# A graph layer on one core: its instruction queues planned with transfers that land later

## The chip, the cores and the metric

The kernel runs on one core of a Trainium2 chip. The core has five instruction queues that matter here: TensorE (PE, with its weight loads, PEld), VectorE (DVE), ScalarE (ACT), GpSimd (POOL) and SyncE (SP, which issues most transfers). The metric is the device time in microseconds (us). Each time given for a kernel is the median of several executions; one more execution, profiled, gives the page and the trace.

## The reference

The reference is one layer of a graph network on 64 graphs of 256 nodes with 256 channels, added to its input:

```
h     = relu(layernorm(x))
x_conv = relu(conv2(relu(conv1(h))) + h)       # over the nodes; conv1 has 1 tap, conv2 17
s     = h @ w_se.T + b_se                      # 3 columns
A     = exp(-|s_n - s_m|^2) * adj
x_nmp = A @ relu(h @ w_msg.T + b_msg)
gi    = [x_conv, x_nmp] @ w_ih.T + b_ih;  gh = h @ w_hh.T + b_hh
r, z  = sigmoid(gi_r + gh_r), sigmoid(gi_z + gh_z)
n     = tanh(gi_n + r * gh_n)
out   = x + (1 - z) * n + z * h
```

The adjacency is 64 x 256 x 256. Everything is float32.

## The kernel before

**Tiling.** The graphs are taken in 32 pairs; four pairs make a block, and there are eight blocks. For a block, the 17-tap convolution is done in a transformed domain: vector instructions (`Fft`, lines 48 to 228) transform the blocks U and V, TensorE multiplies each frequency with a filter matrix (`product`, 935), which a 256 KB transfer from the DRAM tile `filt` brings to one of nine slots `wb0` to `wb8` (`load_kinds`, 910), and vector instructions transform back (`branch_back`, `odd_back`, `q_back`, `p_back`, `join`). The gates of a pair are computed with seven products of quarter matrices instead of eight (`seven`, 1162), whose sums are partly built on TensorE's accumulators by ScalarE and VectorE: `acc<-acc` is line 1167, `acc<-acc,wb` is line 1176, and `wb<-Yv`, `wb<-hT`, `wb<-xnm` are the operand sums of `sums` (1104). Between the two halves of a pair's gates, and around them, stand the steps of other pairs (1426 to 1513).

**Data that arrives by transfer.** Layernorm's statistics of a later pair are taken on VectorE from rows in `x` (`stats`, 745, instruction `st<-x`). Its normalized rows go to `hh` by ScalarE (`turn_h`, 810), are transposed by a transfer into `halves`, sorted back to `hh` by four more (`sort_h`, 821) and copied by ScalarE to a tile of the ring `hT` (`join_h`, 828). The adjacency goes a similar way: `turn_adj` (631), `load_adj` (638) and, on ScalarE, `join_adj` (648) with the copies `adj<-adjh`. A finished pair is transposed by a transfer from `back` to `gn` (`finish`, 1266), copied by ScalarE (`deliver`, 1287, `back<-gn`), and then GpSimd's queue adds the input rows and writes out. So ScalarE's `hT<-hh`, `adj<-adjh` and `back<-gn` and VectorE's `st<-x` each read what a transfer has brought; the other instructions of these two engines mostly feed TensorE.

**What sets the order.** No instruction goes to the chip when its line is run. `Recorder.record` (334) stores it as a task with a planned cost, a transfer's planned share of the DMA engines (`size`), and its predecessors, found from overlapping memory. `plan` (395) then puts the tasks in order, and `emit` (470) issues them in that order, each engine's queue in the order of its own tasks. The program calls `emit` twice: at line 1376 (851 tasks, the first 150 us or so) and at line 1514 (10245 tasks: 4181 tensor, 3106 vector, 2039 scalar, 735 sync, 184 gpsimd).

`plan` gives each task a due time, `late`. TensorE's tasks have theirs from their order in the program, by adding up planned costs; the others' follow backwards from the tasks that need them. Then it plays the engines forward: an engine takes what can start first, and among what can start at that time, the task that is due first. A task can start when its predecessors are done and the lag between the engines has passed. A transfer is taken to move at 1.6 us after its issue or when the DMA engines are through with what was planned before, for `size`, and to be seen 1.1 us after that. At most eight transfers per issuing queue are under way at once in the plan. One rule treats tasks that are not urgent in another way: a transfer of SP whose due time is more than `CALM` = 20 us ahead of TensorE's place in the plan (`pace`) waits until the DMA engines are nearly free.

All instructions pass through `record`, so the profile gives them its line 378 (374 for some joined matmuls), and they are told apart by their tiles.

Of the kernel before, what the change touches and what calls it, by code (L numbers as in the profile page):

```python
# [249 lines left out]
class Recorder:  # L250
# [144 lines left out]
    def plan(self, fixed=False):  # L395

        T, new = self.tasks, range(self.planned, len(self.tasks))
        self.planned = len(T)
        total = 0.0
        for k in new:  # L400
            t = T[k]
            for p in t.preds:
                T[p].succs.append(k)
            if t.engine == "tensor":
                t.late = total
                total += t.cost
        for k in reversed(new):
            t = T[k]
            for s in t.succs:
                t.late = min(t.late, T[s].late - self.lag(t, T[s]) - self.cost(t))  # L410
            if t.first is not None:
                t.late = t.first - 1e6
        ready, free = {e: [] for e in self.LAG}, self.free
        left = {}

        def enable(k):
            at = max((T[p].done + self.lag(T[p], T[k]) for p in T[k].preds), default=0.0)
            ready[T[k].engine].append((at, k))
        for k in new:
            left[k] = sum(p in left for p in T[k].preds)  # L420
            if not left[k]:
                enable(k)
        order = []
        self.pace = 0.0

        def when(e, at, t):
            now = max(free[e], at)
            if t.size:
                now = max(now, self.lanes[e == "gpsimd"][0])
                if e != "gpsimd" and self.pace + self.CALM < t.late < math.inf:  # L430
                    now = max(now, self.dma - 1.0)
            return now

        def commit(k, e, at, now):
            t = T[k]
            ready[e].remove((at, k))
            t.begin = now
            free[e] = t.done = now + t.cost
            if e == "tensor":
                self.pace = max(self.pace, t.late)  # L440
            if t.size:
                if t.cost == self.TURN:
                    free[e] = max(free[e], self.dma + 1.1)
                self.dma = max(self.dma, now + 1.6) + t.size
                t.done = self.dma + 1.1
                lanes = self.lanes[e == "gpsimd"]
                lanes.popleft()
                lanes.append(t.done)
            order.append(k)
            for s in t.succs:  # L450
                left[s] -= 1
                if not left[s]:
                    enable(s)
        while fixed and len(order) < len(new):
            k = new[len(order)]
            e = T[k].engine
            at = next(at for at, j in ready[e] if j == k)
            commit(k, e, at, max(free[e], at, self.lanes[e == "gpsimd"][0] if T[k].size else 0.0))
        while len(order) < len(new):
            best = []  # L460
            for e in ready:
                cand = [(when(e, at, T[k]), T[k].late, k, at) for at, k in ready[e]]
                if cand:
                    now = min(cand)[0]
                    best.append((now, min(c[1:] for c in cand if c[0] <= now + 1e-9), e))
            now, (_, k, at), e = min(best)
            commit(k, e, at, now)
        return order
# [1091 lines left out]
```

## Time and profile before

| | us |
|---|---|
| time, median of 3 executions | 1669.88 (1669.51 to 1676.13) |
| the profiled execution | 1671.57 |
| its span | 1669.8 |
| TensorE busy | 1652.6 (99%) |
| VectorE busy | 1459.3 (87%) |
| ScalarE busy | 1148.6 (69%) |
| GpSimd busy | 242.5 (15%) |

The profiled execution is the slowest core's, and there is only one core. Busy time counts the time in which an engine executes; the ends of matmuls are modelled, so a busy TensorE may still run below its best. In a row of the timeline, the first number is the start, the second the time until the last of the grouped instructions ended, then engine, operation, `out<-in` by tile names and shapes, how many were grouped (`x`), and, in brackets, how long the engine was idle before it and what ended that. 261.39 MB are moved in the span, 157 GB/s on the mean.

### The profile page before, as it was taken

The page shows a single profiled execution, that of the slowest core. Times are in us where ns is not written, and L with a number is a line of the kernel's source. Part 1 is how long each engine was busy: PE and PEld are TensorE (multiplying, and loading weights), DVE is VectorE, ACT ScalarE, POOL GpSimd, SP SyncE. Part 2 cuts the span into 40 slices and gives each one's busy share as a digit, 9 for nine tenths or more (in the row PEclk, how much of TensorE's full clock was granted, in tenths as well). Part 3 has the DMA queues.
Part 4 walks back from the last instruction along what each step waited for, and adds up shares of the span by engine and source line. Part 5 has one row for each costly group of instructions (what it writes and reads, how often), then busy time and mean ns, then how long its engine had stood idle before and what let it go on. Part 6 is the DMA issues. An engine that isn't in the chain of part 4 may idle for free.

```text
span 1669.8 us, 26552 instructions
## 1 busy us (share of the span) xinstructions
PE 1652.6 (99%) x9008; PEld 1417.0 (85%) x9008; DVE 1459.3 (87%) x3391; ACT 1148.6 (69%) x2157; POOL 242.5 (15%) x245
## 2 busy tenths in 40 slices
PE   9999999999999999999999999999999999999999
PEld 6898778988899788988789887898889978898887
DVE  7979979899799997899888997989979899789645
ACT  5556676776767767686676777677676776667655
POOL 4211410013110131102110031001311013000010
PEclk9999999999999999999999999999999999999999
DMA  9982557846578455873568645784647835465022
GB/s 253 312 293 69 105 128 204 262 103 146 118 204 225 101 127 126 240 203 94 101 145 259 158 95 120 177 259 102 148 111 201 240 94 127 110 218 149 19 57 57
DMA packets 314938, 261.39 MB, mean 157 GB/s; under 512 B 192875, under 2 KB 240263, under 8 KB 314802
## 3 DMA queue, kind: packets, MB, share of 16 engines
q1 hardware_dynamic: 297010, 216.71, 49.1%
q0 software_dynamic: 17376, 42.66, 11.1%
q8 instruction: 71, 1.16, 0.3%
q14 instruction: 65, 0.53, 0.1%
q10 hardware_dynamic: 416, 0.32, 0.1%
HBM read 156.60 MB, written 43.78 MB: 120 GB/s over the span
## 4 chain that ended last, share of the span: by engine, by line
PE 79%; DVE 12%; DMA 4%; issue 2%; ACT 1%; SPq 1%; POOL 1%; ACTq 0%; DVEq 0%
PE acc L378 50%; PE aux L378 28%; DVE V L378 3%; DVE T L378 2%; DMA hh<-halves 2%; DVE Yv L378 2%; DVE wb L378 1%; DMA x<-in_x_dram 1%; PE aux L374 1%; DVE e L378 1%; SPq L378 1%; DMA wb<-filt 1%; POOL shift L378 1%; DVE msg L378 1%; DVE st L378 0%
## 5 line engine op out<-in xcount | busy, mean ns | idle before, releaser
L378 PE MATMUL acc<-wb,w_ih 128*128 128x256 f32 x768 | 189.9, 382 | 0.0
L378 PEld LDWEIGHTS acc<-wb,w_ih 128*128 128x128 f32 x768 | 146.0, 191 | 22.1 <-issue 2.3
L378 POOL DMA_DIRECT2D back<-in_x_dram x62 | 56.7, 1059 | 735.1 <-ACT back L378 594.1
L378 POOL TENSOR_TENSOR rstd<-rstd,neg_half 128x4 f32<-128x4 f32 x32 | 79.3, 2478 | 432.4 <-DVE shift L378 275.5
L378 DVE SCALAR_TENSOR_TENSOR V<-T,V 128x128 f32<-128x128 f32 (+2 forms) x448 | 141.5, 384 | 0.0
L378 ACT COPY back<-tr 128x512 uint16<-128x512 uint16 x124 | 130.4, 1078 | 15.7 <-DVE tr L378 15.3
L378 PE MATMUL aux<-wb,w_x 128*128 128x256 f32 x576 | 137.5, 381 | 2.6 <-DVE wb L378 2.6
L378 PE MATMUL acc<-wb,w_x 128*128 128x256 f32 x576 | 135.1, 380 | 0.0
L378 PEld LDWEIGHTS aux<-wb,w_x 128*128 128x128 f32 x576 | 108.7, 190 | 22.6 <-DVE wb L378 5.4
L378 PEld LDWEIGHTS acc<-wb,w_x 128*128 128x128 f32 x576 | 109.0, 190 | 18.6 <-issue 1.9
L378 PEld LDWEIGHTS acc<-U,wb 128*128 128x128 f32 x1024 | 118.3, 192 | 1.8 <-DMA wb<-filt 0.4
L378 PE MATMUL acc<-U,wb 128*128 128x128 f32 x1024 | 119.2, 275 | 0.3 <-DMA wb<-filt 0.3
L378 PE MATMUL aux<-w_msg,hT 128*128 128x259 f32 x512 | 118.6, 381 | 0.0
L378 PE MATMUL acc<-V,wb 128*128 128x128 f32 x1024 | 118.5, 275 | 0.0
L378 PEld LDWEIGHTS acc<-V,wb 128*128 128x128 f32 x1024 | 116.4, 192 | 0.5 <-DMA wb<-filt 0.5
L378 PE MATMUL acc<-wb,w_hh 128*128 128x256 f32 x384 | 105.7, 384 | 5.1 <-DVE acc L378 2.8
L378 DVE TENSOR_TENSOR e<-e,adj 128x256 f32<-128x256 f32 x128 | 68.7, 596 | 46.7 <-ACT e L378 46.7
L378 PEld LDWEIGHTS aux<-w_msg,hT 128*128 128x128 f32 x512 | 95.9, 190 | 14.1
L378 PE MATMUL aux<-hT,w_c 128*128 128x512 f32 x224 | 106.7, 600 | 0.3
L378 PE MATMUL acc<-Yv,w_ih 128*128 128x256 f32 x380 | 103.2, 381 | 2.1 <-ACT Yv L378 2.1
L378 PE MATMUL acc<-hT,w_hh 128*128 128x256 f32 x380 | 105.1, 383 | 0.0
L378 PE MATMUL acc<-xnm,w_ih 128*128 128x256 f32 x380 | 104.0, 380 | 0.0
(218 smaller groups left out, 3909.2 us busy)
## 6 DMA issues: line engine op xcount, KB each, us to landing
wb<-filt SPq DMA_DIRECT2D x348, 256.0 KB
back<-in_x_dram POOLq DMA_DIRECT2D x62, 256.0 KB, 5.3
out_dram<-back POOLq DMA_DIRECT2D x62, 256.0 KB, 3.1
x<-in_x_dram SPq DMA_DIRECT2D x58, 256.0 KB
halves_d<-halves SPq DMA_DIRECT2D x28, 512.0 KB
adjh<-halves_d SPq DMA_DIRECT2D x112, 128.0 KB
hh<-halves SPq DMA_DIRECT2D x108, 128.0 KB
filt<-Yv POOLq DMA_DIRECT2D x18, 224.0 KB, 4.3
```

The lines of the kernel that those rows point to most:

```text
L374: self.tasks[k].call.append(lambda: method(*args, **kw))
L378: self.tasks.append(Task(engine, [lambda: method(*args, **kw)], cost, size, self.first))
```

## The change

The planner's picture of transfers is altered in the second emission only (`new[0]` is the number of the first task of an emission; it is 0 in the first). A transfer is planned as done 2.1 us after its share of the DMA engines, instead of 1.1. And where a task that is no transfer itself has a due time more than 20 us ahead of TensorE's place, at the moment at which its last predecessor is planned, the transfers among its predecessors count as done another 3.0 us later. Nothing else is touched: the same instructions with the same operands are issued, in an order that comes out of the altered plan. Since a planned transfer keeps its place among the eight until it is done, these places are held 1.0 us longer too.

```diff
@@ -414,7 +414,8 @@
         left = {}
 
         def enable(k):
-            at = max((T[p].done + self.lag(T[p], T[k]) for p in T[k].preds), default=0.0)
+            calm = 3.0 if new[0] and not T[k].size and self.pace + self.CALM < T[k].late < math.inf else 0.0
+            at = max((T[p].done + (calm if T[p].size else self.lag(T[p], T[k])) for p in T[k].preds), default=0.0)
             ready[T[k].engine].append((at, k))
         for k in new:
             left[k] = sum(p in left for p in T[k].preds)
@@ -442,7 +443,7 @@
                 if t.cost == self.TURN:
                     free[e] = max(free[e], self.dma + 1.1)
                 self.dma = max(self.dma, now + 1.6) + t.size
-                t.done = self.dma + 1.1
+                t.done = self.dma + (2.1 if new[0] else 1.1)
                 lanes = self.lanes[e == "gpsimd"]
                 lanes.popleft()
                 lanes.append(t.done)
```

## The prediction

> **What bounds the kernel now.** Read first: the busy row of the page and the shares of the chain that ended last.
>
> ```profile
> PE   1652.6 (99%) x9008; PEld 1417.0 (85%) x9008; DVE 1459.3 (87%) x3391; ACT 1148.6 (69%) x2157; POOL 242.5 (15%) x245
> PE 79%; DVE 12%; DMA 4%; issue 2%; ACT 1%; SPq 1%; POOL 1%; ACTq 0%; DVEq 0%
> ```
>
> TensorE is busy for 1652.6 of 1669.8 us, and the change adds and removes no instruction. So it can only win or lose the time in which TensorE stands still or runs slowly. DVE at 87% and ACT at 69% matter only where TensorE waits for them. Which waits involve data that lands late? The list of waits:
>
> ```profile
> ACT back L378 <- DMA gn<-back: 16.3, 10, 3.1
> DVE st L378 <- DMA x<-in_x_dram: 12.3, 9, 3.9
> ACT hT L378 <- DMA hh<-halves: 4.8, 6, 1.7
> PE acc L378 <- DVE acc L378: 2.8, 3, 1.9
> PE aux L378 <- DVE wb L378: 2.6, 6, 0.5
> PE acc L378 <- ACT acc L378: 2.4, 1, 2.4
> ```
>
> The columns are total us, times, longest. DVE and ACT wait for transfers; TensorE hardly waits for transfers, but waits for DVE and ACT. The timeline joins the two. Near 812 us, DVE and then PE:
>
> ```profile
> 809.83 0.43 DVE L378 BATCH_NORM_STATS2 st<-x 128x6 f32<-128x256 f32 x1 [2.68 <-DMA x<-in_x_dram]
> 811.57 0.69 DVE L378 SCALAR_TENSOR_TENSOR acc<-acc,wb 128x512 f32<-128x512 f32 x1
> ```
>
> ```profile
> 809.40 1.02 PE L378 MATMUL aux<-hT,w_c 128*128 128x512 f32 x2
> 812.32 0.70 PE L378 MATMUL acc<-wb,w_hh 128*128 128x256 f32 x2 [1.90 <-DVE acc L378]
> 814.18 1.06 PE L378 MATMUL aux<-hT,w_c 128*128 128x512 f32 x1
> ```
>
> A statistics instruction whose result is wanted in a much later pair heads DVE's queue, waits 2.68 us for its rows, and `acc<-acc,wb`, which TensorE wants at once, stands behind it. Then a second price: at 809.40 two 512-wide matmuls take 1.02 us, at 814.18 one takes 1.06. The windows (us, busy time of PE, PEld, DVE, ACT, POOL, then granted clock, DMA share, GB/s) show why:
>
> ```profile
> 200.00:212.00 12.00, 9.61 (x38) 7.80 (x38) 11.68 (x38) 9.55 (x17) 5.73 (x4) 0.88 0.65 121
> 812.00:820.00 8.00, 7.68 (x25) 5.23 (x26) 7.70 (x17) 4.37 (x11) 0.00 (x0) 0.79 0.64 123
> ```
>
> The granted clock is 0.79 over 8 us after that stall, so (1 - 0.79) x 8 = 1.7 us of clock at most. The same on ACT near 208 us:
>
> ```profile
> 199.44 1.35 ACT L378 COPY back<-gn 128x1024 uint16<-128x1024 uint16 x1 [1.60 <-DMA gn<-back]
> 202.54 1.36 ACT L378 COPY hT<-hh 128x1024 uint16<-128x1024 uint16 x1 [1.74 <-DMA hh<-halves]
> 203.75 0.68 ACT L378 ACTIVATE tr<-acc,b_rz 128x512 f32<-128x512 f32 x1
> 207.38 0.60 ACT L378 ACTIVATE acc<-acc 128x512 f32<-128x512 f32 x1
> ```
>
> Two copies of landed data wait 1.60 and 1.74 us; `acc<-acc`, for which TensorE stands from 205.4 to 208.0, comes after them. A small form recurs in every block of four pairs, some 199 us apart (ACT, DVE and PE near 551 us):
>
> ```profile
> 532.00 1.36 ACT L378 COPY hT<-hh 128x1024 uint16<-128x1024 uint16 x1 [0.69 <-DMA hh<-halves]
> ```
>
> ```profile
> 550.32 0.69 DVE L378 TENSOR_TENSOR wb<-Yv 128x512 f32<-128x512 f32 x1
> ```
>
> ```profile
> 551.07 1.13 PE L378 MATMUL aux<-wb,w_x 128*128 128x256 f32 x4 [0.52 <-DVE wb L378]
> ```
>
> **The size of what can be had.** I took each matmul's distance from the end of the one before and subtracted the median distance of its shape. What is left above that, at places over 0.3 us after the first emission: 2.66 at 208.0; 0.47 at 415.0; 2.17 at 812.3, then 0.42, 0.43 and 0.35 in the slow clock; 0.91 at 1012.9; 2.36 and 0.57 at 1541.7; and eight small ones at 544.5, 551.1, 748.4, 943.7, 950.3, 1148.8, 1340.5, 1347.1 (0.36 + 0.78 + 0.55 + 0.37 + 0.78 + 0.78 + 0.37 + 0.78 = 4.77). All together 15.1 us, 0.9% of the kernel.
>
> **What the Trainium skill says.** "TensorE: Matmul & The Clock Gate", section "Architectural detail", has ScalarE and VectorE take their queues strictly in order: the trace agrees, 2.68 us of waiting passed on to the instruction behind. Its section "What's actually happening" has the clock fall to half for a window of 3413 ns after too little activity: three spells of half clock, 3.413 us each, start at 209.1, 813.2 and 1543.7, each just behind a stall of over 2 us; stalls under 1 us have none. "DMA: Bandwidth & Descriptors", section "Latency and other measured facts", puts the access time of HBM at 0.2 us on average and 2 us under high load, so that a fixed landing time in a plan must be wrong at times: the rows for 809.83 were issued at 802.5, 7.3 us before, with the DMA engines 91% busy.
>
> **The change, part by part.** In the second emission (after about 150 us) the plan lets every transfer land 1.0 us later, and lets an instruction whose due time is more than 20 us away count the transfer 3.0 us later still. Only orders change; no wait is added but what the new orders bring. Laid side by side, the lists of the two kernels differ in place for 1298 of 3106 vector, 1074 of 2039 scalar, 440 of 735 sync, 536 of 4181 tensor and 26 of 184 gpsimd tasks. The 4.0 us of both together exceed every wait in the three DMA rows above (3.9, 3.1, 1.7).
>
> *812 and 1013 us.* The statistics and two transform steps move 24 DVE places back, behind the n gate's chain; `acc<-acc,wb` now follows one sum. It could start by about 809.8, when PE has just issued its last ready matmul: stall gone (2.17), and the slow clock with it (0.42 + 0.43 + 0.35 = 1.20). At 1012.9 the 1.42 us wait of the same statistics is replaced likewise: 0.91. Sum -4.3. The statistics run later, but their result feeds a pair that is tens of us away. At 415 the order is as before: 0.
>
> *208 us.* `tr<-acc,b_rz` (its operand is ready at 199.35) moves ahead of the copies: 199.4 to 200.6. The hT copy still waits to 202.54, then 1.36 + 0.64 (message relu, moved forward) + 1.34 + 1.35 less overlaps of 0.1 each: `acc<-acc` starts near 207.1 and ends 207.7, only 0.3 earlier; PE has one more conv1 matmul pair (0.86 us) to fill with. Between 1.1 (stall shortened) and 2.66 + 1.5 of clock (gone): I take 1.3, since the wait for hh stays.
>
> *Every block.* The hT copies move 28 and 15 ACT places back, one adj copy and one back copy 20; the copies V<-acc and the exponentials come first. Taking out the 0.69 wait and the 1.36 copy ahead of V<-acc, DVE's back transform starts near 536.4 instead of 537.7 and `wb<-Yv` ends near 549.5 instead of 551.0, while PE wants it at 550.3. I take 4.0 of the 4.77, as 1 in 6 may stay. hT is first wanted by matmuls tens of us after (its copy would end by about 543), which hides the move; without that cover each late copy costs up to 1.36.
>
> *SP.* Four hh loads (0.6 us of issue each) move 6 places back behind filter loads, and transpositions (3.75 us of issue) 8; the filter loads move 1 to 3 places forward and none gets a new long wait in front. adjh loads move 10 to 20 back. POOL: two places at most. I price this at 0; if a filter load were delayed, its cover is 7.2 us (issued 521.67, used 528.84).
>
> *1541 us.* Orders nearly equal from 1510 on: 0.
>
> *New stalls.* 1298 moved DVE tasks at 87% load will not all be free. Bounds: 0, and 1.2 us in each of seven blocks (the slower rival). I take +1.5.
>
> Sum: -4.3 - 1.3 - 4.0 + 1.5 = -8.1. The profiled execution took 1671.57 us (span 1669.8 and 1.8 around it) and would take 1663.5; the median of the three runs is 1669.88, 1.7 less, so **1661.8**.
>
> **Rivals.** (a) *Most of the moves reorder hidden work.* Only the two statistics stalls go (-4.3) and new small ones give 1 to 3 back: 1666 to 1669. For it: DVE's 87% leave it little room to catch up within a block. (b) *No effect*: the real landings, not the planned order, set the waits, and the instructions merely wait in other places: 1669.9. Against: the waiting instruction does stand 24 places later. (c) *Slower: SP's queue.* The hT copies leave hh about 12 us later, so the next fill of hh and its transposition wait on SP (the profile has SP waiting 111.4 us for ACT's hh in 15 places, up to 15.5), with filter loads behind them. The cover of a filter load is 7.2 us, of which its own landing takes about 3 (an estimate from the page's 3.1 us median for the equally large out_dram writes); a transposition of 3.75 us in front uses up the rest. Beyond that each us of delay is a us of TensorE, once in each of seven blocks. From 8.1 / 7 = 1.2 us per block it eats the gain; at 2.4 it gives 1669.9 - 8.1 + 16.8 = 1678.6. Against: filter loads stand earlier in SP's list, not later. (d) *All goes*, clock spells at 208 and 812 included: -4.3 - 4.2 - 4.8 = 1656.6.
>
> **From cases to numbers.** A difference of 0.5% (8.3 us, so 1661.5 and 1678.2) is about what a measurement of this kernel tells from none: the three runs lie within 0.4%. Chances: my forecast (most stalls go, own range 1657 to 1666) 0.56, (d) 0.09, (a) 0.15, (b) 0.07, (c) or a like new stall 0.13. The forecast's centre lies just on the faster bound, so somewhat under six tenths of it count as faster: 0.56 x 0.58 + 0.09 = 0.42; slower takes most of (c), 0.10, and same the rest, 0.48. The range 1656 to 1674 leaves out the low end of (d) and the strong half of (c).
>
> **What would show it.** Right: the wait of st for x and of ACT's copies shrink to a few us; PE shows no wait at 812, 1013, 551, 748, 950, 1148, 1347; no clock under 0.9 around 812; 208 shorter; 1541 unchanged. Wrong: a new PE wait in every block (for DVE wb, ACT h or DMA wb), more SP wait for ACT hh, or the same statistics wait with TensorE behind it at another time.

## The result, and the profile after

The changed kernel takes 1657.57 us (median of four executions, 1654.78 to 1658.67), the kernel before, with the runs of that session, 1672.91 us (1669.51 to 1676.13). The ratio is 0.9906, 95% interval 0.9877 to 0.9935: faster by 0.9%. The profiled execution took 1657.88 us with a span of 1656.1, 13.7 us less than before.

The page of the changed kernel, busy row and shares of the chain that ended last:

```profile
PE 1645.5 (99%) x9008; PEld 1416.7 (86%) x9008; DVE 1458.7 (88%) x3391; ACT 1150.6 (69%) x2157; POOL 242.6 (15%) x245
PE 96%; DVE 2%; DMA 2%; ACT 0%; issue 0%; SPq 0%; DVEq 0%; ACTq 0%
```

The work is the same (9008 matmul records, 3391 on DVE, 2157 on ACT). The chain went from PE 79% and DVE 12% to PE 96% and DVE 2%: it now hardly ever leaves TensorE. From the list of waits of the changed kernel (total us, times, longest), the rows on late data and TensorE's own:

```profile
ACT back L378 <- DMA gn<-back: 17.0, 8, 2.5
DVE st L378 <- DMA x<-in_x_dram: 4.0, 2, 3.6
PE acc L378 <- ACT Yv L378: 2.1, 1, 2.1
PE acc L378 <- DMA wb<-filt: 1.2, 2, 1.0
ACT hT L378 <- DMA hh<-halves: 0.7, 1, 0.7
PE aux L378 <- DVE wb L378: 0.3, 1, 0.3
```

Two of the three DMA rows shrank (st from 12.3 to 4.0, both of these waits before 350 us; hT from 4.8 to 0.7). The third did not: ACT still waits 17.0 us for `gn<-back`, before 16.3. But TensorE's rows for DVE acc and ACT acc are gone, and its row for DVE wb fell from 2.6 to 0.3. ScalarE's waits for `gn` no longer have anything urgent behind them, and cost TensorE nothing here. The place that was at 812 us, now at 802, DVE and then PE:

```profile
801.65 0.68 DVE L378 TENSOR_TENSOR wb<-hT 128x512 f32<-128x512 f32 x1
802.25 0.69 DVE L378 SCALAR_TENSOR_TENSOR acc<-acc,wb 128x512 f32<-128x512 f32 x1
```

```profile
802.85 0.59 PE L378 MATMUL aux<-Yv,w_x 128*128 128x256 f32 x2
803.28 0.59 PE L378 MATMUL acc<-wb,w_hh 128*128 128x256 f32 x2
```

No statistics stand ahead of `acc<-acc,wb`; the matmul that needs it starts 0.43 us after the one before, its usual spacing. Near 208 us, ScalarE:

```profile
200.91 0.69 ACT L378 ACTIVATE tr<-acc,b_rz 128x512 f32<-128x512 f32 x1 [1.80 <-issue]
202.84 1.35 ACT L378 COPY hT<-hh 128x1024 uint16<-128x1024 uint16 x1 [0.66 <-DMA hh<-halves]
206.99 0.63 ACT L378 ACTIVATE acc<-acc 128x512 f32<-128x512 f32 x1
```

The gate activation goes ahead of the hT copy, as forecast, and `acc<-acc` still ends only at 207.6. The windows of these two places:

```profile
200.00:212.00 12.00, 12.00 (x54) 9.91 (x53) 12.00 (x41) 9.45 (x16) 3.09 (x4) 1.00 0.50 113
798.00:806.00 8.00, 8.00 (x35) 6.32 (x34) 8.00 (x19) 3.40 (x8) 0.56 (x1) 1.00 0.86 223
```

PE is busy throughout and the granted clock is 1.00 (0.88 and 0.79 before).

**Where the 13.7 us are.** The measure of the prediction (each matmul's distance from the end of the one before, less the median of its shape, summed over distances more than 20 ns above it) gives, by stretch of the span:

| excess, us | to 150 | 150 to 1500 | from 1500 | sum |
|---|---|---|---|---|
| before | 6.9 | 32.7 | 6.7 | 46.2 |
| changed | 8.0 | 17.9 | 6.7 | 32.5 |

All the gain, 14.8 us, lies between 150 and 1500 us, and there not one place of the changed kernel is over 0.3 us above its own matmuls' spacing, small joined ones apart; what is left, about 0.6 us per 50, is mainly these (`aux<-zT`, the same in both kernels). By place: 812 with its clock 3.4, 1013 0.9, 415 0.5, the eight small ones of the blocks 4.8, the 50 us from 200 on 4.2: 13.8, and 1 us of smaller ones. The stretch to 150 us is the first emission, whose plan the change doesn't touch; its 1.1 us more are late filter loads, which differ from run to run (6.5 to 9.5 us in eleven of thirteen profiles).

### The profile page after: what moved, and what is told of

The parts are those of the page before. It is cut to its first block, busy times and chain, and to the rows that moved or that the text cites. A ratio compares the mean times of both kernels' runs of the same rounds, so it can differ in the third digit from the quotient of the medians.

```text
span 1656.1 us, 26512 instructions
## 1 busy us (share of the span) xinstructions
PE 1645.5 (99%) x9008; PEld 1416.7 (86%) x9008; DVE 1458.7 (88%) x3391; ACT 1150.6 (69%) x2157; POOL 242.6 (15%) x245
## 4 chain that ended last, share of the span: by engine, by line
PE 96%; DVE 2%; DMA 2%; ACT 0%; issue 0%; SPq 0%; DVEq 0%; ACTq 0%
PE acc L378 58%; PE aux L378 37%; DMA wb<-filt 1%; PE aux L374 1%; DVE V L378 0%; DVE T L378 0%; DMA T<-in_x_dram 0%; DVE st L378 0%; DVE Yv L378 0%; DVE wb L378 0%; ACT h L378 0%; DVE e L378 0%; ACT Sv L378 0%; ACT T L378 0%; DVE hh L378 0%
## 5 line engine op out<-in xcount | busy, mean ns | idle before, releaser
L378 POOL TENSOR_TENSOR rstd<-rstd,neg_half 128x4 f32<-128x4 f32 x32 | 75.7, 2366 | 399.3 <-DVE shift L378 261.2
L378 PEld LDWEIGHTS aux<-wb,w_x 128*128 128x128 f32 x576 | 108.9, 191 | 15.7 <-DVE wb L378 1.0
L378 PE MATMUL aux<-e,msg 128*128 128x256 f32 x448 | 104.7, 379 | 0.0
```

The source lines that it names most:

```text
L378: self.tasks.append(Task(engine, [lambda: method(*args, **kw)], cost, size, self.first))
```

## The experiments

The table gives the time, the ratio to the kernel before, run beside it on the same chip, and the excess of TensorE between 150 and 1500 us. The kernel before has 32.7 there and the changed one 17.9.

| kernel | median us | ratio, 95% interval | excess 150 to 1500 |
|---|---|---|---|
| only statistics put back | 1665.82 | 0.9958 (0.9940 to 0.9977) | 25.1 |
| only row loads put forward | 1668.20 | 0.9965 (0.9948 to 0.9982) | 24.4 |
| landing alone | 1658.82 | 0.9905 (0.9874 to 0.9937) | 20.2 |
| 3.0 us for what is not urgent, alone | 1664.94 | 0.9954 (0.9934 to 0.9974) | 24.6 |
| ACT's order alone | 1727.52 | 1.0316 (1.0277 to 1.0355) | 81.6 |
| ACT's and DVE's order | 1685.99 | 1.0072 (1.0049 to 1.0095) | 47.1 |
| ACT's, DVE's and PE's order | 1658.46 | 0.9907 (0.9884 to 0.9931) | 18.5 |
| changed, landing 3.1 | 1661.10 | 0.9926 (0.9898 to 0.9953) | 23.6 |
| changed, last block edited, first try | 1657.82 | 0.9908 (0.9888 to 0.9927) | 17.9 |
| changed, last block edited, mended | 1656.79 | 0.9902 (0.9887 to 0.9916) | 17.7 |

One more kernel, with extra instructions that make stalls of known length, was executed once, with the profiler (1683.48 us). It is read by its trace alone and has no row in the table.

In several of these kernels, the second emission makes both plans and takes each engine's queue from one of them; the queues are then issued in any order that keeps the predecessors:

```diff
+        for self.soft in (False, True):
...
+            order = self.plan()
+            for e in self.LAG:
+                if self.soft == (e in self.TAKE):
+                    queues[e] = [k for k in order if self.tasks[k].engine == e]
...
+        self.edit(queues)
```

`soft` switches the two edits of the change; `TAKE` names the engines that get the changed kernel's order.

**Theory A**: a transfer that lands later than planned stops the instruction that reads it; this one stands at the head of an in-order queue, and what TensorE needs stands behind. **Rival B**: the new orders of TensorE and of the transfers carry the gain.

### Moving one kind of reader, or one kind of transfer

The queues of the kernel before, first with five statistics instructions moved, then with six pairs of transfers swapped:

```diff
+        q = queues["vector"]
...
+            if self.op[q[n]][0] == "bn_stats" and op == "scalar_tensor_tensor" and out.tensor.space == bass.MemoryType.PSUM:
+                q.insert(n + 24, q.pop(n))
```

```diff
+        q = queues["sync"]
...
+            if name[n:n + 7] == ["turn halves", "x"] + 4 * ["hh"] + ["x"]:
+                q[n], q[n + 1] = q[n + 1], q[n]
```

> All five queues in the order of the kernel before; only in VectorE's, the first statistics of a pair moves 24 places back wherever the sum acc<-acc,wb stands four places behind it (five places in the kernel: near 412, 610, 810, 1010 and 1208 us). Theory A (a late landing is passed on to TensorE through the head of an in-order queue): the stalls at 415 (0.47), 812 (2.17, and 1.20 of slow clock) and 1013 (0.91) go, 4.8 us, ratio 0.9971; the stalls at 208 and in every block (551 and its like) stay. Rival B (the gain comes from the new orders of TensorE and SP, and the waits of VectorE are only a symptom): no change, ratio 1.000, or the statistics wait turns up elsewhere.

> All five queues in the order of the kernel before, but in SP's the first load of the rows x is put ahead of the transposition of hh instead of behind it (six places, the five of the statistics runs among them). The row loads then start 4 to 5 us earlier; VectorE's queue is untouched. Theory A (the lateness of the load is what is passed on): the statistics' waits of 0.7 to 2.7 us at 412 to 1208 go, with them the stalls at 415, 812 (and its slow clock) and 1013, as with the statistics put back: 4.8 us, ratio 0.996 to 0.997. Rival (it is the place in VectorE's queue as such that costs, or the transposition delayed by 0.65 us costs as much): no change or slower, 1.000 or more.

Both do what theory A says: the stalls at 415, 812 and 1013 are gone, the ratios are 0.9958 and 0.9965 against 0.9971 and 0.996 to 0.997 expected; the stalls of the blocks stay. The two kernels have one thing in common, that the statistics' data are there when their turn comes. With the loads put forward, DVE's queue is that of before, statistics ahead of `acc<-acc,wb`, and runs through (SP's and DVE's timelines):

```profile
794.67 0.61 SPq L379 DMA_DIRECT2D x<-in_x_dram  x1
797.58 4.43 SPq L379 DMA_TRANSPOSE halves<-hh  x1
```

```profile
806.84 0.43 DVE L379 BATCH_NORM_STATS2 st<-x 128x6 f32<-128x256 f32 x1
808.58 0.70 DVE L379 SCALAR_TENSOR_TENSOR acc<-acc,wb 128x512 f32<-128x512 f32 x1
```

So the place in VectorE's queue as such costs nothing; the late landing passed on does. The medians fell by 5.3 and 5.4 us, the profiled spans by 6.5 and 6.8, more than the 4.8 expected. One part is that in these two executions the stall at 208 (2.81 and 3.07 us) was not followed by half clock, as it was before (1.3 to 1.5 us of excess less; see the last section); the rest lies in smaller places. These two runs test the statistics alone. No run moved only ScalarE's copies within the old orders, so for the stalls of the blocks and at 208 theory A rests on the traces and on the mixed queues below.

### Each half of the change alone

```diff
-            calm = 3.0 if new[0] and not T[k].size and self.pace + self.CALM < T[k].late < math.inf else 0.0
+            calm = 0.0
```

```diff
-                t.done = self.dma + (2.1 if new[0] else 1.1)
+                t.done = self.dma + 1.1
```

> Only the landing of 2.1 instead of 1.1 us in the plan, without the 3.0 us for instructions not needed soon. In the order that comes out, statistics still stand ahead of acc<-acc,wb at the place of 812 us, and a back copy ahead of the gate activations at 208 us; V<-acc stands ahead of the hT copies. Theory A: the block stalls go (4 to 5 us), 812 and 208 stay, ratio 0.997 to 0.998. Rival B or any theory in which the landing is the better half: ratio under 0.993.

> Only the 3.0 us for instructions not needed soon; the landing stays 1.1 us. In its order the statistics stand 23 places behind acc<-acc,wb, at 208 us the gate activations come first, and V<-acc comes ahead of the hT copies. Theory A: all of the changed kernel's gain within 1.5 us, ratio 0.990 to 0.992, no stall over 0.3 us between 150 and 1500 us. Rival: the two halves add up, so that this one alone gives half or less, ratio 0.995.

Both expectations of theory A failed in their sizes, and both numbers are those that I had set for the rivals. The landing alone has all of the gain as far as the times can tell (0.9905; by the excess 12.5 of 14.8 us), the 3.0 us alone half of it (0.9954). The two do not add up, since either removes most of the same stalls. The traces say why. In the landing's kernel the statistics do stand ahead of `acc<-acc,wb` at this place, but they don't wait, because SP issues the row loads before the transposition. SP's timelines of the kernel before, and of the landing alone:

```profile
797.80 4.67 SPq L378 DMA_TRANSPOSE halves<-hh  x1
802.51 0.63 SPq L378 DMA_DIRECT2D x<-in_x_dram  x1
```

```profile
791.27 0.60 SPq L378 DMA_DIRECT2D x<-in_x_dram  x1
794.18 0.65 SPq L378 DMA_DIRECT2D x<-in_x_dram  x1
797.04 4.30 SPq L378 DMA_TRANSPOSE halves<-hh  x1
```

The loads are 11 us earlier there. I had looked only at where the reader stood. The plan has a second way to deal with a load that lands later, which is to issue it sooner; the landing takes this one, the 3.0 us takes the other, and at 812 either is enough. The 3.0 us alone clears the blocks, 812 and 1013 as well, but makes one new stall near 210 us (ScalarE, then PE):

```profile
207.49 1.33 ACT L378 COPY hT<-hh 128x1024 uint16<-128x1024 uint16 x1 [4.85 <-DMA hh<-halves]
```

```profile
210.68 2.07 PE L378 MATMUL aux<-hT,w_c 128*128 128x512 f32 x2 [3.30 <-ACT hT L378]
```

Its hh loads were issued at 201.5, after a wait of SP of 15.8 us for ScalarE's hh; in the changed kernel they were issued at 197.2. With the half clock behind it the 50 us from 200 on have 5.5 us of excess where the changed kernel has 0.8, most of the 5.4 us between their spans. Why the hh activations come late in that one order was not tried further.

### Queues of one plan mixed with those of the other

> ScalarE's queue in the order of the changed kernel, the four others in the order of the kernel before. Theory A: the eight small stalls of the blocks (4.8 us in all) go, since V<-acc and the exponentials no longer stand behind the hT copy; 812, 1013 and 415 stay with their clock; 208 is shortened by 0.4 at most, since TensorE has no other matmul there. Sum 4 to 5 us, ratio 0.9972. Rival B: no change, 1.000. Rival D (ScalarE's order is what matters everywhere, the statistics come along): 812 goes too, ratio 0.993.

> ScalarE's and VectorE's queues in the order of the changed kernel, TensorE's, SP's and GpSimd's in that of the kernel before. If the loss of the run with ScalarE's order alone (1727.5 us) comes from ScalarE and VectorE handing each other work in two different orders, the loss goes here: ratio 0.992 to 1.000. If it comes from ScalarE running ahead of SP's transfers, it stays: over 1.02.

> The three computing engines in the order of the changed kernel; SP's and GpSimd's queues in that of the kernel before. Theory A (what counts is where the readers of transfers stand): the gain of the changed kernel to within 2 us, ratio 0.990 to 0.993. Rival (the new order of the transfers on SP carries the gain, as with the row loads that the landing alone put forward): half of the gain or less, ratio over 0.995.

The three together settle rival B's part on the transfers: with SP's and GpSimd's queues as before, the gain is whole (0.9907, excess 18.5). The row loads are sooner there too, at 399.88 us where the kernel before has 407.11, though SP's order is the old one: they stand behind the transposition, which waits for ScalarE's hh, and ScalarE writes hh sooner. The two others failed against all that I expected: ScalarE's order alone costs 3.2%, and with VectorE's it still costs 0.7%. Here a whole queue taken from the other plan was worse than the old one until the orders planned with it came along. With ScalarE's and VectorE's order but TensorE's old one, the stalls at 544 and 551 are gone (none over 0.3 us between 480 and 620), but a new one of 1.7 us stands in each block, for instance here (PE, then ACT):

```profile
642.67 1.46 PE L379 MATMUL aux<-wb,w_x 128*128 128x256 f32 x6
645.56 0.70 PE L379 MATMUL acc<-wb,w_hh 128*128 128x256 f32 x2 [1.43 <-ACT acc L379]
```

```profile
643.70 1.32 ACT L379 COPY back<-gn 128x1024 uint16<-128x1024 uint16 x1
644.88 0.63 ACT L379 ACTIVATE acc<-acc 128x512 f32<-128x512 f32 x1
```

ScalarE has two copies of 1.3 us in front of `acc<-acc`. In the changed kernel it has them too, but TensorE has six matmul records of another pair in between:

```profile
635.23 1.46 PE L378 MATMUL aux<-wb,w_x 128*128 128x256 f32 x6
636.52 1.46 PE L378 MATMUL aux<-e,msg 128*128 128x256 f32 x6
637.82 0.59 PE L378 MATMUL acc<-wb,w_hh 128*128 128x256 f32 x2
```

So rival B is half right: TensorE's new order is needed beside the new orders of ScalarE and VectorE, as filler for what ScalarE now does in between; SP's is not needed. For ScalarE's order alone, statistics waits of up to 5.4 us came back (19.4 us in 7) along with 22.6 us of TensorE waiting for `acc<-acc`; which of these starts the loss was not taken apart.

### Still later landings

```diff
-                t.done = self.dma + (2.1 if new[0] else 1.1)
+                t.done = self.dma + (3.1 if new[0] else 1.1)
```

> The changed kernel with 3.1 instead of 2.1 us for the planned landing. Theory A: there is hardly a stall left between 150 and 1500 us, so a still later landing can gain nothing; with places among the eight held longer it orders more work behind transfers than need be. Between 0 and 10 us slower than the changed kernel, ratio 0.991 to 0.997. Rival (later is better still, since the longest waits of ScalarE and VectorE for transfers were 3.1 to 3.9 us): ratio under 0.989.

As theory A has it: 0.9926, 3.5 us slower than the changed kernel by the medians, with new stalls of 1.79 us at 193.6, 0.88 at 211.7, and 0.45 once in each of five blocks. The intervals of the two ratios overlap, but no two executions do: 1660.14 us and more here, 1658.67 and less there. Later is not better.

### The price of a stall

```diff
+            if op == "scalar_tensor_tensor" and out.tensor.space == bass.MemoryType.PSUM and "acc" in out.tensor.name:
+                for _ in range({19: 3, 27: 5, 35: 7, 43: 9, 51: 12}.get(sums, 0)):
+                    self.nc.vector.bn_stats(*self.idle)
+                sums += 1
```

> The changed kernel, with 3, 5, 7, 9 and 12 extra statistics instructions (128 x 256, 0.33 us each by their spacing, output not used) put into VectorE's queue ahead of acc<-acc,wb at the same place of five successive blocks, 605 to 1392 us; there TensorE has 0.34 us to spare. Stalls of about 0.65, 1.3, 2.0, 2.6 and 3.6 us, 10.2 in sum. Theory of the clock: a stall under 1 us costs itself alone, one over 2 us costs 1.2 to 1.7 us more in half clock; in sum 13 to 16 us, and the point lies between the second and the third. Rival: stalls are caught up later in the block, or the slow clock at 812 had another cause: 10 us or less and no half clock.

One extra instruction took 0.46 us and not 0.33, so the stalls are larger: 1.07, 1.99, 2.92, 4.15 and 5.53 us. Windows around the second, third and fifth of them (us, busy time of PE, PEld, DVE, ACT, POOL, granted clock, DMA share, GB/s):

```profile
807.00:815.00 8.00, 6.28 (x24) 4.27 (x24) 7.86 (x19) 2.64 (x7) 0.00 (x0) 1.00 0.51 151
1006.00:1018.00 12.00, 9.35 (x29) 5.77 (x29) 10.68 (x25) 4.32 (x9) 0.35 (x1) 0.86 0.71 192
1409.00:1425.00 16.00, 11.05 (x34) 7.12 (x33) 13.95 (x32) 5.12 (x10) 0.00 (x0) 0.79 0.53 136
```

The first two cost no clock, the third and fourth 1.7 us each ((1 - 0.86) x 12), the fifth 3.4, two spells. The 50 us around each have 1.2, 2.4, 4.7, 5.5 and 7.6 us more excess than the 0.6 of their neighbours, 21.4 in sum for 15.7 of stalls: a stall is not caught up later, and the third costs 1.6 times itself. So the sum came out above the 13 to 16 us expected because the stalls were longer, and the step in the price lies between the second and the third, as expected.

### The last block

The one stall that the change left stands in the last block, at 1541.7 before and 1528.0 after, 2.36 us in both: TensorE waits for `Yv`, with no work of a next block to fill in. It is a chain of VectorE and ScalarE, not a transfer. I moved 20 tasks that are not urgent in it (message sums, one other sum, transpositions, `z`, `zT`) behind it:

```diff
+        back("vector", {10509, 10515, 10518, 10474}, 10485)
+        back("tensor", {10525, 10526}, 10571)
+        back("scalar", {10519, 10520, 10521, 10522}, 10486)
+        back("scalar", {10524, *range(10527, 10536)}, 10572)
```

> The changed kernel with 35 tasks of the last block reordered: on VectorE three msg sums and one wb sum move behind the two Yv scalings, on TensorE two transpositions move behind the Yv matmuls that wait, on ScalarE the z and zT copies move behind the two Yv activations. In the changed kernel TensorE stands there at 1528.0 for 2.36 us and once more for 0.7, and the clock is 0.98 over the 90 us around it (1.8 us). Moving 1.3 us of VectorE's work away should leave a stall of 1.1. If the clock falls only behind stalls of about 2 us or more, the edit saves 1.3 for the stall and 1.2 to 1.8 for the clock: 2.5 to 3 us, ratio to the kernel before about 0.989, and no half clock near 1528. Rival: the clock falls anyway (another cause, such as few matmuls per us in that stretch), the saving is 1.3 at most.

The expectation failed, by the very mechanism of this study. One message activation, task 10523, was left ahead of the `Yv` activations and waited for the sums that had been moved back; TensorE's stall grew to 3.3 us (ScalarE's timeline; then the second edit against the first):

```profile
1527.48 0.63 ACT L379 ACTIVATE msg<-msg 128x512 f32<-128x512 f32 x1 [3.62 <-DVE msg L379]
1528.01 1.32 ACT L379 ACTIVATE Yv<-Yv,bn_shift 128x512 f32<-128x512 f32 x2
```

```diff
-        back("vector", {10509, 10515, 10518, 10474}, 10485)
-        back("tensor", {10525, 10526}, 10571)
-        back("scalar", {10519, 10520, 10521, 10522}, 10486)
-        back("scalar", {10524, *range(10527, 10536)}, 10572)
+        back("vector", {10509, 10515}, 10485)
+        back("vector", {10536}, 10515)
+        back("vector", {10518, 10474}, 10536)
+        back("tensor", {10525, 10526}, 10583)
+        back("scalar", {*range(10519, 10525), *range(10527, 10536)}, 10572)
```

> The edit of the last block mended: in the first one a msg activation was left ahead of the two Yv activations on ScalarE and waited 3.6 us for the msg sums that had been moved back, so TensorE's stall grew to 3.3 us. Now it stands behind them too, with the z and zT copies, and wb<-Yv comes after two msg sums instead of after seven instructions. By hand: TensorE stands about 1.3 to 1.5 us near 1527 and 0.4 to 0.8 after it, where the changed kernel has 2.36 and 0.68. If half clock needs a stall of about 2 us, the clock stays at 1.00 and 2 to 3 us are saved against the changed kernel; if the clock falls anyway, under 1.2. In the ratio to the kernel before this is 0.989 against 0.9906, within the intervals, so the profile has to decide.

Mended, the stall is 1.49 us, with 0.53 behind it (PE, and the window of the last block):

```profile
1528.28 1.13 PE L379 MATMUL acc<-Yv,w_ih 128*128 128x256 f32 x4 [1.22 <-ACT Yv L379]
```

```profile
1510.00:1600.00 90.00, 88.20 (x440) 75.88 (x440) 63.09 (x119) 60.27 (x124) 5.88 (x8) 1.00 0.22 42
```

The clock is 1.00 and the excess from 1500 us on falls from 6.7 to 4.9 us, a little under what was expected, as two stalls of 0.3 and 0.5 us came in behind. Some 1.5 us of these 1.8 are the clock: the two kernels with one half of the change have the old last block and its stall of 2.36 us, but no half clock behind it, and 5.2 us of excess there. So the mended order saves this in those executions only in which half clock would have followed (see the last section). Its ratio, 0.9902 (0.9887 to 0.9916), is the lowest of all; that it is faster than the changed kernel rests on that stretch of one trace alone, since the two intervals overlap.

## Why the prediction was right

The time lies inside the range (1656 to 1674), 4.2 us under the forecast of 1661.8, and the kernel is faster by more than 0.5%, to which I gave 0.42 and to no change 0.48: the range held, the likeliest class by my own chances did not come. What happened is nearest to rival (d), that all goes, at 1656.6, which had 0.09.

- **What bounds it; the size to be had**: right. The gain is TensorE's stalls and the clock behind them, and came to about the 15.1 us listed, less the end of the kernel (2.9), plus the clock at 208.
- **812 and 1013** (-4.3): right in size and mechanism (in the changed kernel the statistics run at 814.8, 12.6 us behind the sum); both single edits of the queues before confirm it.
- **415** (0, "the order is as before"): wrong, 0.5 us. VectorE's order there is indeed the same. But SP issues the row loads at 395.31 instead of 407.11, ahead of the transposition, and the statistics no longer wait. The step failed because it looked at the reader and not at the load.
- **208** (-1.3): the term was mis-sized; 4.2 us went. The worked end of `acc<-acc`, 207.7, was right to 0.1 us, but that is luck. The kernel as a whole came to this place 1.3 us later, after a filter load at 111.5 that happened to be late: the matmuls ahead of the stall (`aux<-wb,w_x`) start at 205.46, before at 204.18. Counted from them, three things took 2.5 of the 2.66 us. The hT copy starts 2.62 us ahead of them instead of 1.64, because ScalarE's last `hh<-x,shift,rstd` ends 15.7 us ahead instead of 14.2, and so the transposition and the hh loads go out sooner; I had taken the landing as fixed at 202.54. From this copy to `acc<-acc` it is 4.15 us instead of 4.84. The pair of conv1 matmuls adds 0.86 of work. The late filter load is not what hid the stall: the two kernels of the first experiment have the old order here, came as late (205.36 and 205.97), and stalled for 2.81 and 3.07; the two kernels with the last block edited have the new order here, came at 205.79 and 206.98 with the copy at 203.24 and 204.32, and have no stall over 0.3. The landing is not fixed in one order either: in the kernel with the extra instructions, with the new order here too, the copy starts only 2.07 us ahead (207.74 and 209.81), and 0.7 us of stall is left.
- **Every block** (-4.0 of 4.8): all 4.8 went; the copies' move is as worked, V<-acc ahead of hT (changed kernel, ScalarE; before, the copy at 532.00 stood ahead):

```profile
528.28 1.07 ACT L378 COPY V<-acc 128x512 f32<-128x512 f32 x2 [0.94 <-PE acc L378]
532.34 0.66 ACT L378 COPY V<-acc 128x256 f32<-128x256 f32 x2
532.86 1.38 ACT L378 COPY hT<-hh 128x1024 uint16<-128x1024 uint16 x1
```

- **SP** (0): right by the run with SP's queue as before. The slower rival (c) didn't come: SP's wait for ACT's hh fell from 111.4 us to 41.4 instead of growing. Its wait for ACT's adj did grow, from 81.5 to 229.5, but the list shows no matmul that waits for a filter load after 150 us.
- **New stalls** (+1.5): none. This allowance (1.5) and the 208 term (2.9), with 0.8 in the blocks, 0.5 at 415 and the 1.0 of smaller places, less the 1.1 us lost before 150 us, are the 5.6 us between forecast and profiled execution (1663.5 and 1657.88).
- **What would show it**: the waits of st shrank as said; those of ACT's copies of gn did not (16.3 to 17.0), yet the stalls they had passed on are gone.

## What to carry to other kernels

Where engines take their queues in order, look for a wait on a transfer whose result is not needed soon, and at what stands behind it: the price is on the instruction behind, and it goes either by issuing the load sooner or by letting the reader stand later. Plan a landing with some margin, but not with the most that was ever seen (2.1 us was better than 1.1 and than 3.1 here). Take the orders of several queues from one plan: moving five or six instructions by hand within one queue gained 0.4% here, but one whole queue, or two, out of the better plan were slower than the old one.

## What the runs showed of the hardware

- **Half clock goes by fixed windows: where a stall lies counts, beside its length.** In thirteen profiles there are 54 stalls of TensorE of more than 1.3 us after the first 60 us. Of the 26 of up to 1.99 us, 25 left the clock at 1.00 (the other followed 2 us after another stall). Of the 21 from 2.1 to 3.1 us, 12 were followed by half clock and 9 not; all 7 of 3.2 us or more were, the two longest by two spells. The Trainium skill, "TensorE: Matmul & The Clock Gate", section "What's actually happening", says that the window of 3413 ns runs freely. The traces agree: within each profile the spells start a whole number of 3.413 us apart (in the kernel before at 209.08, 813.24 and 1543.69, which is 177.0 and 214.0 windows). If the profiles are cut into windows by these starts and TensorE's idle time in each is added up from the matmul records, after the first 60 us all 17 windows with 1.98 us or more were followed by half clock; of the 9 with 1.71 to 1.96 us, 4; of the 6077 with less, one (1.53 us, itself at half clock). The ends of matmuls are modelled, so these bounds are rough.
- **This explains what looks like chance.** The stall of 2.36 us in the last block is the same in eleven profiles; in the seven where half clock followed, one window had 1.71 to 2.28 us idle, in the other four at most 1.47 to 1.96. The stalls of 2.81 and 3.07 us at 208 were split by a window's end, 1.93 and 1.84 at most. In the mended last block no place of the windows would put more than 1.48 us into one, so by this rule the shorter stall is enough to keep the clock up there. My sharp point of about 2 us of stall, in the expectations of the last block, was too simple.
- **Seven statistics instructions in a row that wrote one and the same tile took 3.20 us**, 0.46 each. In the kernel's own statistics, where each writes its own columns, four take 1.40 us, 0.33 apart. Their input is another tile too. Which of the two is the cause was not tried.
